# A fused cross-attention and mixture layer: attention probabilities transposed on VectorE in 32x32 blocks instead of on TensorE, with the softmax run one pair of heads ahead

## The chip, the cores and the metric

The kernel runs on one core of one Trainium2 chip. The metric is device time in microseconds (us), the median of three runs. A separate execution of the same program, recorded by the hardware profiler, gives the views quoted below. Engines are named as in the profile: PE is TensorE, PEld its weight loads, DVE is VectorE, ACT is ScalarE, POOL is GpSimd, SP is SyncE, which here only issues DMAs.

## What is computed

```
x: (16, 64, 512)   ctx: (16, 64, 512)   fside: (16, 32, 64, 64)   mask: (16, 64, 64)   all float32 but the mask
n = layernorm(x);  q = n @ Wq;  k = ctx @ Wk;  v = ctx @ Wv          # 32 heads of 128
score = q k^T / sqrt(128) + fside;  masked;  probs = softmax(score)   # 64x64 for each of 16 samples and 32 heads
x = x + (probs @ v) @ Wo
x = x + layernorm(x) @ base_W^T + base_b + routed low-rank term       # 8 experts of rank 16
```

There are 16 samples of 64 tokens, so 1024 rows. The reference works in float32, and the kernel keeps that accuracy with split operands: each operand of a large product is written as hi + lo, and each product is three matmuls (hi*hi, hi*lo, lo*hi).

## The kernel before, in words

**Stages.** Up to about 329 us the kernel makes all keys and values, with a Winograd-like scheme that forms a 2x2 block product from seven sub-products (`winograd`, L207), and stores them in DRAM (`kd`, `vd`). Then comes the attention loop over 16 pairs of heads (NP = 16), from 329 to about 728 us. The last stage is the dense layer with its router.

**The step strings.** In the attention loop the order of TensorE's work is written out by hand, one letter for a step:

- Q is one of the seven sub-products of the queries of the *next* pair (six 512-column matmuls, `Queries.run`, L514 to L538). Sub-products 1, 6, 7 and 4 add up in one PSUM bank, x, and after each of them ScalarE copies the bank out (`u`, L530, or `q`, L533) before the next of them may write it. Sub-product 2 has bank z; 5 and 3 share bank y. VectorE adds the copies to z or y (`q`, L537).
- S is the scores of both heads of a pair (`scores`, L455): 64 recorded matmuls, then for each head on VectorE scale and bias (L465) and the negated maximum (L467), on ScalarE eight exponentials with their sums (L470), and on VectorE the reciprocal and the normalising product (L473 to L475). A pair's two heads are called A and B below.
- T turns one head's probabilities: four TensorE transposes of 128x128 into a bank (L481) and a ScalarE copy into SBUF (`pt`, L484).
- O is one of the eight token blocks of the output projection of the *previous* pair (six 512-column matmuls, `proj_o`, L501), added to the accumulator `acc` by VectorE (L510).

Between the strings stands the product of probabilities and values (`pv_mm`, L487), called PV here: 128 recorded small matmuls for both heads into four banks, each bank then split by ScalarE (`oh`, L70) and VectorE (`ol`, L71). The strings are "QSQQQQQTQT" for the first pair, "QSQQOOQOQOOQOQOTTO" for the middle ones and "SOOOOOOTOT" for the last. A pair's probabilities are thus used in the same turn in which they are made.

**What sets the order.** On each engine instructions run in the order fixed when the program is built; a scheduler places them by priority and dependence, and an instruction that waits holds everything behind it on its engine. SP issues all loads in one such queue: keys (`load_k`, L426), values (`load_v`, L433), Wo (`load_o`, L440), the side bias (`bias_of`, L450), Wq (`load_pair`, L413). GpSimd adds the mask to the bias (L453) and forms sums of Wq blocks (L161). Buffers come from tagged pools whose sizes are in BLOCKS (L40): `sn` (8) holds `u`, `p` and `pt`, `v` (5) the value blocks. There are six large PSUM banks (`psp`) and two small ones (`pss`), which hold the scores and the transposes.

**After the loop** the weights of the dense layer are split into hi and lo (`bh`, `bl`, `lbh`, `lbl`, L70 and L71).

Of the kernel before, what the change touches and what calls it, by code (L numbers as in the profile page):

```python
# [9 lines left out]
F32 = mybir.dt.float32  # L10
# [9 lines left out]
P = 128  # L20
D = 512
# [17 lines left out]
ORDER_1 = (1, 6, 5, 7, 2, 4, 3)  # L39
BLOCKS = dict(raw=10, g=18, sum=4, sn=8, ob=8, v=5, bm=2, o=9)  # L40
BIG = 1.0e30
# [6 lines left out]
def xattn_ffn_kernel(ctx: ExitStack, tc: tile.TileContext, x, ctxT, wq, wk, wv, wo, fside, mask,  # L48
# [20 lines left out]
    def split(hi, lo, src, lo_eng=None):  # L69
        nc.scalar.copy(hi, src)  # L70
        (lo_eng or nc.vector).tensor_tensor(lo, src, hi.bitcast(F32), ALU.subtract)  # L71

# [36 lines left out]
    with ExitStack() as actx:  # L109
# [6 lines left out]
        def small_bank(name):  # L116
            return pss.tile([P, 512], F32, tag="s", name=name)
# [208 lines left out]
        def x_turn(t, xn):  # L326
            ps = small_bank("pst")
            transposed(ps, xn)
            b, g = divmod(t, 4)
            dst = xT.rearrange("p k (g a b s) -> p g b k a s", g=4, a=2, b=2)[:, g, b]  # L330
            nc.scalar.copy(dst, ps.rearrange("p (k a s) -> p k a s", k=KC, a=2))

# [14 lines left out]
        with tc.manual_schedule(engines={nc.tensor.engine}):  # L347
# [75 lines left out]
            def gran_q(rq, order):  # L423
                return Weights(rq[0][:, 0], rq[0][:, 1], rq[1][:, 0], rq[1][:, 1], P, nc.gpsimd).all(order)

            def load_k(h):  # L426
                kT = []
                for j in range(2):
                    kT.append(blk("raw", "kT"))
                    nc.sync.dma_start(out=kT[j], in_=kd[h][:, j * HALF:(j + 1) * HALF])  # L430
                return kT
# [24 lines left out]
            def scores(qT, kT, bm):  # L456
                ps = small_bank("pss").rearrange("p (t s) -> p t s", t=NT)
                for t in range(NT):
                    for a in range(2):
                        n = 4 * (t // 2) + 2 * a + t % 2  # L460
                        c = slice((n % 8) * S, (n % 8 + 1) * S)
                        nc.tensor.matmul(ps[a * S:(a + 1) * S, t, :], lhsT=qT[n // 8][:, c],  # L462
                                         rhs=kT[n // 8][:, c], start=True, stop=True)
                p = blk("sn", "p", F32, (P, NT, S))
                nc.vector.scalar_tensor_tensor(p, ps, scale, bm, ALU.mult, ALU.add)  # L465
                nm = sm.tile([P, NT], F32, tag="nm", name="nm")
                nc.vector.tensor_reduce(nm, p, AX.X, ALU.max, negate=True)  # L467
                sme = sm.tile([P, NT], F32, tag="sme", name="sme")
                for t in range(NT):
                    nc.scalar.activation(p[:, t, :], p[:, t, :], AF.Exp, bias=nm[:, t:t + 1],  # L470
                                         accum_out=sme[:, t:t + 1])
                rc = sm.tile([P, NT], F32, tag="rc", name="rc")
                nc.vector.reciprocal(rc, sme)  # L473
                nc.vector.tensor_tensor(rc, rc, valid, ALU.mult)  # L474
                nc.vector.tensor_tensor(p, p, rc.unsqueeze(2).to_broadcast([P, NT, S]), ALU.mult)  # L475
                return p

            def transpose_p(p):
                ps = small_bank("pst")
                for g in range(4):  # L480
                    nc.tensor.transpose(ps[:, g * P:(g + 1) * P],  # L481
                                        p[:, 2 * g:2 * g + 2, :].rearrange("p t k -> p (t k)"), ident)
                pt = blk("sn", "pt", F32, (P, NT, S))
                nc.scalar.copy(pt, ps.rearrange("p (u q) -> p u q", q=S))  # L484
                return pt

            def pv_mm(i, pt, v, home="o"):  # L487
                ps = [bank() for _ in range(2)]
                for u in range(NT):
                    for b in range(2):  # L490
                        r = slice(b * S, (b + 1) * S)
                        for d in range(0, P, S):
                            c = slice(i * P + d, i * P + d + S)
                            nc.tensor.matmul(ps[b][d:d + S, u * S:(u + 1) * S], lhsT=v[u // 2][r, u % 2, c],  # L494
                                             rhs=pt[r, u, :], start=True, stop=True)
                res = []
                for b in range(2):
                    hl = [blk(home, f"o{c}", F32R) for c in "hl"]
                    split(hl[0], hl[1], ps[b])
                    res.append(hl)  # L500
                return res  # L501

            def proj_o(t, cts, w):
                ps = bank()
                b, g = divmod(t, 4)
                c = slice(g * P, (g + 1) * P)
                for i, ct in enumerate(cts):
                    mm3(ps, [a[:, c] for a in ct[b]], w[i], i == 0, i == 1)
                with tc.high_priority(offset=SOON):
                    nc.vector.tensor_tensor(acc[:, t, :], acc[:, t, :], ps, ALU.add)  # L510

            class Queries:
# [6 lines left out]
                def run(self, g, order):  # L519
                    mm = mm_weights(tx, g)  # L520
                    b, s = {}, {}
                    for i in order:
                        x_ = "x" if i in (1, 6, 7, 4) else "z" if i == 2 else "y"
                        if i in (1, 2, 5):
                            b[x_] = bank()
                        mm(i, 0, b[x_], i in (1, 2, 5))
                        with tc.high_priority(offset=SOON):
                            if i in (1, 6, 7):
                                s[i] = blk("sn", "u")
                                nc.scalar.copy(s[i], b["x"])  # L530
                            if i == 4:
                                self.blocks[1, 0] = blk("ob", "q21")
                                nc.scalar.copy(self.blocks[1, 0], b["x"])  # L533
                            for at, key, u, bk in ((2, (0, 0), 1, "z"), (7, (1, 1), 7, "y"), (3, (0, 1), 6, "y")):
                                if i == at:
                                    self.blocks[key] = blk("ob", "q")
                                    nc.vector.tensor_tensor(self.blocks[key], s[u], b[bk], ALU.add)  # L537
                        yield  # L538
# [22 lines left out]
            NP = H // 2  # L561
            pts = v = w = prev = None
            for p in range(NP):
                last = p + 1 == NP
                if pts is not None:
                    prev = ([pv_mm(i, pts[i], v) for i in range(2)], w)
                v = load_v(p)
                after = None
                steps = "SOOOOOOTOT" if last else "QSQQOOQOQOOQOQOTTO" if p else "QSQQQQQTQT"
                pts, t, n = [], 0, 0  # L570
                for c in steps:
                    if c == "S":
                        ps = [scores(qs.head(i), ks[i], bms[i]) for i in range(2)]
                        if not last:
                            ks = [load_k(2 * p + 2 + i) for i in range(2)]
                            bms = [bias_of(2 * p + 2 + i) for i in range(2)]
                    elif c == "Q":
                        nxt(1)
                        n += 1
                        if n == 3:  # L580
                            w = load_o(p)
                        if n == 7 and p + 2 < NP:
                            after = Queries(load_pair(p + 2), ORDER)
                        if n == 7 and p + 2 == NP:
# [7 lines left out]
                            for kc in range(KC):  # L592
                                nc.sync.dma_start(out=sbw[kc], in_=base_wT[:, kc])
                    elif c == "T":
                        pts.append(transpose_p(ps[len(pts)]))
                    else:
                        proj_o(t, *prev)
                        t += 1
                        if last and t == 2:
                            w = load_o(p)  # L600
                qs, nxt = nxt, after
            now = ([pv_mm(i, pts[i], v, "g") for i in range(2)], w)
            proj_o(t, *prev)
# [10 lines left out]
    bl = fw.tile([P, KC, NF], F32R, name="bl")  # L614
    for i in range(2):
        split(bh[:, 2 * i:2 * i + 2, 0:NB], bl[:, 2 * i:2 * i + 2, 0:NB], sar[i])
    for kc in range(KC):
        split(bh[:, kc, NB:NF], bl[:, kc, NB:NF], sbw[kc])
    lbh = fw.tile([P, NF], F32R, name="lbh")
# [202 lines left out]
```

## Time and profile before

| What | Value |
|---|---|
| Median of three runs | 777.97 us (777.95 to 778.37) |
| The profiled execution's own time | 779.41 us |
| Span of its records | 777.6 us |
| Granted TensorE clock | 0.997 of full |
| One middle pair, from S to the next S | 25.81 us (371.20, 397.01 and 422.82 us in the chain) |
| PE busy | 770.8 us |
| DVE, ACT, POOL busy | 574.3, 413.6, 134.9 us |
| DMA engines' mean share | 46.7% |

The span begins with the first recorded instruction and ends with the last. Busy time is the union of an engine's records, waits left out. Matmuls are pipelined, so a record of 390 ns starts about 227 ns after the one before it; what a matmul costs TensorE is this distance, not its record.

### The profile page before, as it was taken

The numbers are of one execution on the slowest core, as the hardware profiler recorded it, in microseconds if no ns is written. First come the engines' busy times: TensorE is split into PE (matmuls) and PEld (weight loads), VectorE is DVE, ScalarE is ACT, GpSimd is POOL, SyncE is SP. The second block draws the span as 40 slices with busy tenths as digits, with TensorE's granted clock in tenths as the row PEclk, the third lists the DMA queues.
The fourth block names the chain that finished last, engine by engine and source line by source line (L and its number), as shares of the span: only waits on it lengthen the run. The fifth ranks groups of instructions, "written<-read, shape, count | busy, mean of one in ns | idle before, by whom it ended". The sixth has DMA issues, their size and how long they took to land.

```text
span 777.6 us, 16694 instructions
## 1 busy us (share of the span) xinstructions
PE 770.8 (99%) x6314; PEld 642.1 (83%) x6314; DVE 574.3 (74%) x1036; ACT 413.6 (53%) x1165; POOL 134.9 (17%) x143
## 2 busy tenths in 40 slices
PE   8999999999999999999999999999999999999998
PEld 6888887888888888887888888888888888888898
DVE  6986666665665756787877787778777877779875
ACT  5664454545454545575564556455645564556461
POOL 0000000000000522133330332033203320310330
PEclk9999999999999999999999999999999999999999
DMA  6695646464536345474554355435543544352011
GB/s 243 227 294 179 195 161 209 131 208 151 203 120 204 122 140 200 166 243 140 185 164 122 110 178 165 129 104 176 164 138 96 176 164 131 103 176 70 1 53 58
DMA packets 74705, 120.48 MB, mean 155 GB/s; under 512 B 7680, under 2 KB 24832, under 8 KB 74624
## 3 DMA queue, kind: packets, MB, share of 16 engines
q1 hardware_dynamic: 74480, 119.36, 46.7%
q8 instruction: 49, 0.80, 0.4%
q14 instruction: 32, 0.26, 0.1%
q10 hardware_dynamic: 144, 0.06, 0.0%
HBM read 83.74 MB, written 35.65 MB: 154 GB/s over the span
## 4 chain that ended last, share of the span: by engine, by line
PE 95%; DVE 3%; ACT 1%; DMA 1%; issue 0%; POOL 0%; SPq 0%; DVEq 0%; ACTq 0%; POOLq 0%
PE ps L259 74%; PE yz L259 5%; PE ps L668 5%; PE pss L462 4%; PE ps L494 4%; PE pst L481 2%; DVE gl L71 1%; ACT p L470 1%; DMA cT<-in_ctxT 1%; PE pst L104 0%; DVE bs L634 0%; DVE wl L71 0%; PE pt L104 0%; DVE ol L71 0%; DVE acc L510 0%
## 5 line engine op out<-in xcount | busy, mean ns | idle before, releaser
L70 ACT CAST gh<-s 128x512 fp32r<-128x512 f32 (+1 forms) x128 | 65.6, 515 | 121.1 <-PE ps L259 112.3
L470 ACT ACTIVATE p<-p,nm 128x64 f32<-128x64 f32 x256 | 85.5, 336 | 31.3 <-DVE nm L467 31.3
L259 PE MATMUL ps<-wh,oh 128*128 128x512 f32 x256 | 101.3, 396 | 0.0
L510 DVE TENSOR_TENSOR acc<-acc,ps 128x512 f32<-128x512 f32 x128 | 85.9, 681 | 20.2 <-PE ps L259 20.0
L259 PE MATMUL ps<-wh,ol 128*128 128x512 f32 x256 | 99.8, 390 | 0.0
L259 PE MATMUL ps<-wl,oh 128*128 128x512 f32 x256 | 99.8, 390 | 0.0
L71 DVE TENSOR_TENSOR gl<-s,gh 128x512 fp32r<-128x512 f32 (+1 forms) x128 | 71.5, 562 | 32.9 <-ACT gh L70 31.8
L161 POOL TENSOR_TENSOR s<-rq 128x256 f32<-128x256 f32 x32 | 27.6, 863 | 262.8 <-DMA rq<-in_wq 127.9
L71 DVE TENSOR_TENSOR gl<-raw,gh 128x512 fp32r<-128x512 f32 x48 | 34.5, 722 | 36.5 <-ACT gh L70 26.1
L259 PEld LDWEIGHTS ps<-wl,oh 128*128 128x128 f32 x256 | 48.0, 188 | 10.0
L259 PEld LDWEIGHTS ps<-wh,ol 128*128 128x128 f32 x256 | 48.1, 188 | 9.7 <-DVE ol L71 0.4
L259 PEld LDWEIGHTS ps<-wh,oh 128*128 128x128 f32 x256 | 48.1, 188 | 9.5
L70 ACT CAST gh<-raw 128x512 fp32r<-128x512 f32 x48 | 29.7, 622 | 48.3 <-PE yz L259 29.3
L453 POOL TENSOR_TENSOR bm<-bm,maskb 128x512 f32<-128x512 f32 x32 | 48.2, 1526 | 28.9 <-DVE rc L474 21.5
L470 ACT ACTIVATION_READ_ACCUMULATOR p<-p,nm 128x1 f32 x256 | 48.2, 188 | 0.0
L71 DVE TENSOR_TENSOR ol<-ps,oh 128x512 fp32r<-128x512 f32 x64 | 39.9, 682 | 10.3 <-ACT oh L70 10.3
L96 POOL TENSOR_TENSOR rs<-rs,nhalf 128x1 f32<-128x1 f32 x8 | 4.4, 551 | 246.1 <-DVE rs L95 246.1
L537 DVE TENSOR_TENSOR q<-u,ps 128x512 f32<-128x512 f32 x48 | 32.6, 680 | 9.2 <-PE ps L259 8.9
L70 ACT CAST oh<-ps 128x512 fp32r<-128x512 f32 x64 | 33.2, 591 | 11.6 <-PE ps L494 11.6
L71 DVE TENSOR_TENSOR gl<-rq,gh 128x256 fp32r<-128x256 f32 x48 | 26.9, 562 | 15.4 <-ACT gh L70 15.4
L462 PEld LDWEIGHTS pss<-kT,q 128*64 128x64 f32 x1024 | 31.3, 138 | 5.7 <-PE ps L259 5.2
L475 DVE TENSOR_TENSOR p<-p,rc 128x512 f32<-128x512 f32 x32 | 34.9, 1092 | 1.1
(260 smaller groups left out, 2015.8 us busy)
## 6 DMA issues: line engine op xcount, KB each, us to landing
kd<-c SPq DMA_DIRECT2D x64, 256.0 KB, 2.2
vd<-c SPq DMA_DIRECT2D x64, 256.0 KB, 2.6
kT<-kd SPq DMA_DIRECT2D x64, 256.0 KB, 5.0
v<-vd SPq DMA_DIRECT2D x64, 256.0 KB, 4.3
raw<-in_wk SPq DMA_DIRECT2D x32, 256.0 KB, 4.0
raw<-in_wv SPq DMA_DIRECT2D x32, 256.0 KB, 4.1
rq<-in_wq SPq DMA_DIRECT2D x32, 256.0 KB, 4.7
bm<-in_fside SPq DMA_DIRECT2D x32, 256.0 KB, 5.0
```

The lines of the kernel that those rows point to most:

```text
L70: nc.scalar.copy(hi, src)
L71: (lo_eng or nc.vector).tensor_tensor(lo, src, hi.bitcast(F32), ALU.subtract)
L161: self.eng.tensor_tensor(r, a, b, op)
L259: nc.tensor.matmul(o, lhsT=a, rhs=b, start=first and n == 0, stop=last and n == 2, skip_group_check=True)
L453: nc.gpsimd.tensor_tensor(bm, bm, maskb, ALU.add)
L462: nc.tensor.matmul(ps[a * S:(a + 1) * S, t, :], lhsT=qT[n // 8][:, c], rhs=kT[n // 8][:, c], start=True, stop=True)
L470: nc.scalar.activation(p[:, t, :], p[:, t, :], AF.Exp, bias=nm[:, t:t + 1], accum_out=sme[:, t:t + 1])
L475: nc.vector.tensor_tensor(p, p, rc.unsqueeze(2).to_broadcast([P, NT, S]), ALU.mult)
L494: nc.tensor.matmul(ps[b][d:d + S, u * S:(u + 1) * S], lhsT=v[u // 2][r, u % 2, c], rhs=pt[r, u, :], start=True, stop=True)
L510: nc.vector.tensor_tensor(acc[:, t, :], acc[:, t, :], ps, ALU.add)
L537: nc.vector.tensor_tensor(self.blocks[key], s[u], b[bk], ALU.add)
L668: nc.tensor.matmul(o, lhsT=a, rhs=b, start=start, stop=stop, skip_group_check=True)
```

## The change

- **The turn.** TensorE's transposes and the copy out of PSUM are gone. `turned_p` now makes one VectorE transpose per head that turns each 32x32 block in place (`pb`), then one ScalarE copy of the whole of `pb` into `pt`, then four SBUF-to-SBUF DMAs of 32 partitions x 1 KB that put the two off-diagonal blocks of each half where they belong.
- **The tokens.** So that each half of the partitions holds one sample, the order of tokens in `x`, `ctx` and the output is changed on the host side, and the indexing in `x_turn`, `scores` and `pv_mm` follows. The number and size of these instructions stay.
- **The order.** `scores` is cut into `scores`, `exps` and `normed`. In the step strings the scores of a pair now come at the top of a turn, PV (letter P) is inside the string and uses the probabilities made in the turn before, h stands for normalising and turning one head, e for one head's exponentials, and a small o for a projection step of the pair before the previous one. New ordering edges (`issue_after`) put groups of instructions behind others on the same engine: Wo's split behind the split of PV's banks, the second head's exponentials behind the copy of sub-product 7, the dense layer's weight splits behind the turn of pair 14's last head. The splits of PV's banks get high priority.
- **Buffers.** `sn` grows from 8 to 9, `v` shrinks from 5 to 4.

Matmul records fall by 128 and SP's DMA issues rise by 128; VectorE has 32 transposes more, ScalarE has as many instructions as before.

```diff
-BLOCKS = dict(raw=10, g=18, sum=4, sn=8, ob=8, v=5, bm=2, o=9)
+BLOCKS = dict(raw=10, g=18, sum=4, sn=9, ob=8, v=4, bm=2, o=9)
...
-            def transpose_p(p):
-                ps = small_bank("pst")
-                for g in range(4):
-                    nc.tensor.transpose(ps[:, g * P:(g + 1) * P],
-                                        p[:, 2 * g:2 * g + 2, :].rearrange("p t k -> p (t k)"), ident)
-                pt = blk("sn", "pt", F32, (P, NT, S))
-                nc.scalar.copy(pt, ps.rearrange("p (u q) -> p u q", q=S))
+            def turned_p(p):
+                pb = blk("sn", "pb", F32, (P, 2, NT, 32))
+                turned[:] = [nc.vector.transpose(pb, p.rearrange("p t (b k) -> p b t k", b=2))]
+                pt = blk("sn", "pt", F32, (P, 2, NT, 32))
+                turned.append(nc.scalar.copy(pt, pb))
+                with tc.issue_after(loaded[-1].ins):
+                    for r in (0, S):
+                        for a in range(2):
+                            to, at = r + 32 * (1 - a), r + 32 * a
+                            nc.sync.dma_start(out=pt[to:to + 32, a], in_=pb[at:at + 32, 1 - a])
                 return pt
...
-                steps = "SOOOOOOTOT" if last else "QSQQOOQOQOOQOQOTTO" if p else "QSQQQQQTQT"
+                steps = ("QSQQQQQQ" if p == 0 else "SQQQPQQOOQOhOQOOOO" if p + 2 < NP else
+                         "SQQQPQQQQOhSeeOOOOOh" if p + 1 < NP else "PoohOOOOOOO")
...
+                    if c == "P":
+                        old, told = prev, t
+                        prev, t = ([pv_mm(i, pts[i], v, "g" if p + 1 == NP else "o") for i in range(2)], w), 0
+                        del pts[:2]
+                        v = load_v(p)
+                    elif c == "S":
+                        ss += [scores(pairs[ns].head(i), ks[i], bms[i]) for i in range(2)]
+                        ns += 1
...
+                        if p == ns - 1:
+                            exps_of(1 if p else 2)
+                        if p == 0:
+                            soften()
+                            soften()
                     elif c == "Q":
+                        nxt = pairs[p + 1]
                         nxt(1)
                         n += 1
-                        if n == 3:
-                            w = load_o(p)
+                        if n == 5 and ss:
+                            with tc.issue_after(nxt.third):
+                                exps_of(1)
+                                soften(nxt.last)
+                        if n == 5:
+                            with ExitStack() as behind:
+                                for e in [e.ins for e in evicted] or [nxt.first]:
+                                    behind.enter_context(tc.issue_after(e))
+                                w = load_o(p)
...
+                    elif c == "h":
+                        soften(added.ins)
+                    elif c == "e":
+                        behind = list(turned)
+                        with tc.issue_after(turned[1].ins):
+                            exps_of(1)
+                    elif c == "o":
+                        added = proj_o(told, *old)
+                        told += 1
...
+    with tc.issue_after(behind[0].ins), tc.issue_after(behind[1].ins):
+        for i in range(2):
+            split(bh[:, 2 * i:2 * i + 2, 0:NB], bl[:, 2 * i:2 * i + 2, 0:NB], sar[i])
```

`exps_of(n)` runs the exponentials of n heads that wait in `ss`; `soften` runs `normed` and `turned_p` for the next head.

## The prediction

> **What bounds the kernel now.** I read first the busy line and the shares of the chain that ended last.
>
> ```profile
> PE 770.8 (99%) x6314; PEld 642.1 (83%) x6314; DVE 574.3 (74%) x1036; ACT 413.6 (53%) x1165; POOL 134.9 (17%) x143
> ...
> PE 95%; DVE 3%; ACT 1%; DMA 1%; issue 0%; POOL 0%; SPq 0%; DVEq 0%; ACTq 0%; POOLq 0%
> ```
>
> TensorE is busy for all but 7 us, and the chain runs through it. So work taken from TensorE is worth its full time if nothing makes TensorE wait afterwards. Next the chain through one middle pair (start, length, what):
>
> ```profile
> 391.14 0.87 PE pst L481 x8
> 392.02 1.38 PE ps L259 x6
> 393.39 2.02 PE ps L494 x128
> 395.42 1.59 PE ps L259 x6
> 397.01 2.02 PE pss L462 x64
> 399.02 17.93 PE ps L259 x78
> 416.96 0.87 PE pst L481 x8
> ```
>
> The pair takes 25.81 us, with no other engine in the chain. The eight transposes take 0.87 us, a step of six large matmuls 1.36 to 1.38. The engine's waits add one thing, TensorE's only wait in the whole attention loop, at 361.6 us:
>
> ```profile
> PE ps L259 <- DVE q L537: 0.7, 1, 0.7
> ```
>
> Then the busy time by stage, one pair (length, then PE, PEld, DVE, ACT, POOL):
>
> ```profile
> 371.20:397.00 25.80, 25.80 (x292) 21.45 (x293) 20.45 (x36) 14.16 (x52) 6.48 (x6) 1.00 0.43 142
> ```
>
> VectorE has 5.3 us to spare in a pair, ScalarE 11.6. Last, ScalarE's timeline in the first pair, and the rows nearest to the new work:
>
> ```profile
> 331.81 0.35 ACT L470 ACTIVATE p<-p,nm 128x64 f32<-128x64 f32 x1 [1.96 <-DVE nm L467]
> ...
> 332.16 0.33 ACT L470 ACTIVATE p<-p,nm 128x64 f32<-128x64 f32 x1
> ...
> 333.16 0.56 ACT L530 COPY u<-ps 128x512 f32<-128x512 f32 x1
> ```
>
> ```profile
> L475 DVE TENSOR_TENSOR p<-p,rc 128x512 f32<-128x512 f32 x32 | 34.9, 1092 | 1.1
> L467 DVE TENSOR_REDUCE nm<-p 128x8 f32<-128x512 f32 x32 | 22.0, 686 | 1.0
> L484 ACT COPY pt<-pst 128x512 f32<-128x512 f32 x32 | 17.4, 587 | 23.6 <-PE pst L481 23.6
> ```
>
> Exponentials start 0.334 us apart. After four of them the copy of a sub-product (u) gets its turn; that interleaving is what keeps TensorE fed there, and it will matter.
>
> [...] the ordinary one-input row here is 686 ns for 512 elements. No transpose on VectorE is in this trace. [...] the same product p<-p,rc takes 0.68 us at best and 1.81 at worst, while GpSimd works.
>
> **The change, part by part.**
>
> *Transposes off TensorE.* The first and last pair spend 2 x 0.44 us on them, the fourteen others 0.87: 0.88 + 0.88 + 14 x 0.87 = 13.9 us saved, switching included, since these are distances along the chain. PV and S still stand between large matmuls as often as before, so no other switch appears. The wait at 361.6 us should go too, because its cause was the crowded second pair: -0.7.
>
> *VectorE transposes.* 32 x 0.69 = 22 us, 1.4 a pair: 20.45 + 1.4 = 21.8 us in a pair of 24.9. Off the path at that price. [...] I take 0.69. [...]
>
> *ScalarE copy.* 0.59 us for each head as now, from SBUF in place of PSUM: nothing.
>
> *DMAs.* Eight a pair, 32 KB each. SP takes 0.32 to 0.4 us to issue one, and the shortest landing on the page is 2.2 us (kd<-c), so a head is home about 4 us after its copy. In the new order they are issued behind the second half of the next keys and one Wo load; what is queued behind them is the other Wo load, needed some 12 us later, and the next pair's Wq, bias and keys, which cannot go before the next S anyway. The later head is turned near 22 us after S, home near 26, used at 31: 5 us of slack. Nothing. In bytes it is 4 MB on 120.
>
> *The tokens, the value buffers.* The same count of instructions; four value blocks are refilled right behind PV, 23 us before use. Nothing.
>
> *The new order in a middle pair.* Counted from S: Q1 at 2.02, Q2 at 3.5, Q6 at 4.87, PV at 6.3, then Q5, Q7, and the first O at 11.2. Two places are tight. Q6 writes bank x again and must wait for the copy of Q1. In the first pair of the kernel before scores started at 329.10, the copy began at 333.16 and took 0.56: 4.62 after S, 0.2 us early, if VectorE is free at 1.2 us. I walked VectorE's order: it has caught up by the seventh O with about 0.5 us to spare, so yes. The first O needs the split of PV's banks; ScalarE begins 1.1 us after PV's start (now 523.58 against 522.46), so VectorE's first split ends near 8.7: early. I allow 0.05 us a pair: +0.6. The bounds are 0 and about 0.3.
>
> *The filling, a new wait.* In the first turn all sixteen exponentials, both copies to pt, two Wo casts and a Wq cast stand ahead of the copy of Q6 on ScalarE; Q7, two steps later on TensorE, waits for that copy. TensorE: S at 329.10, Q6, Q5, ready for Q7 at 333.97. ScalarE: exponentials from 331.81, 16 x 0.334, to 337.15; copy for A 0.5, casts 0.5 + 0.5 + 0.3, to 339.0. Head B meanwhile: last sum ready 337.3, reciprocal and products to about 338.4, one Wo split to 339.05, transpose to 339.75; copy for B to 340.3, then the copy of Q6 to 340.9. TensorE stands from 333.97 to 340.95: +7.0, bounds 6.3 (no VectorE contention) to 9 (GpSimd's bias addition and a slow transpose). Then S of the second pair follows Q3 directly, and its second quarter needs VectorE's sum of Q3, behind two small splits: +0.9 (0.5 to 1.5). Nothing hides these 7.9 us: on TensorE everything stands behind Q7.
>
> *The draining.* In turn 14 Q4 follows Q7 with no O between, while ScalarE still has four splits and two Wo casts ahead of the copy of Q7: ready at 12.0 against 11.2 us after S, +0.8. In turn 15 VectorE also carries six splits of the dense weights (0.4 to 0.7 us each), so PV's split for the first O comes late, about +0.6; and the last head's transpose near 38 us after S of turn 14, plus copy and DMAs, meets the last PV at 40.3 to 41.3, about +1.0. Sum +2.4, bounds 0.8 to 6. The moved splits leave the window 720 to 740 us, where TensorE hardly waits (0.3 us), so nothing comes back.
>
> *Sum*, on the profiled execution: 779.41 - 13.9 - 0.7 + 0.6 + 7.9 + 2.4 = 775.7 us. The runs' median lies 1.44 below that execution, so 777.97 - 3.7 = **774.3 us**.
>
> **The rivals.**
> - *Clean.* Neither filling nor draining costs anything: 777.97 - 13.9 - 0.7 = 763.4. For it: TensorE waits almost nowhere now, and every order is by hand. Against: ScalarE's order in the first turn is fixed, and 16 x 0.334 us cannot shrink.
> - *Slower: VectorE's transpose at half pace.* Each pair has two; at 1.37 us VectorE carries 1.36 us more. Half a us of slack before the seventh O and 0.2 at Q6 absorb 0.6, the rest, 0.73 us, holds Q6 in each of 13 pairs: 9.5 us. With the 0.6 already allowed taken out: 774.3 - 0.6 + 9.5 = 783.2. It decides from about 1.2 us a transpose, where 13 pairs lose 4 us. For it: VectorE stands at 21.8 of 24.9 us already. [...]
> - *A wash.* One cost alone at its upper bound: filling 10.5 us (776.9), draining 6 us (777.9), or 0.3 us lost at Q6 in each of 13 pairs (777.6).
> - That TensorE does the transposes still is excluded: 128 of its matmuls are gone from the changed program.
>
> **How the numbers follow.** Differences within 0.2% (776.4 to 779.5 us) are about what a measurement of this kernel can tell from no change. The forecast, 770 to 776.4: 0.62. Clean or nearly, below 770: 0.10. Wash: 0.14. Slower, above 779.5: 0.14. So faster 0.72, same 0.14, slower 0.14. The range 766 to 780 leaves out about 0.05 below and 0.12 above; the transpose at 1.37 us lies outside it.
>
> **What would show it.** No pst records from L481, and S to S at 24.9 us in the middle pairs. A gap on TensorE of 7 us near 334, ended by ScalarE's copy u, and VectorE's transpose at 0.69 us. If the middle pairs keep a wait at Q6 or at the first O, the walk of VectorE's order is wrong; if the gap near 334 is absent, my reading of ScalarE's order is. If PV waits for a DMA in the middle pairs, the slack of 5 us was wrong.

## The result and the profile after

| | before | after |
|---|---|---|
| Median | 778.27 us (777.47 to 779.87, 21 runs) | 776.67 us (775.14 to 778.86, 21 runs) |
| Ratio | | 0.998, 95% interval 0.9972 to 0.9987 |
| Span of the profiled execution | 777.6 us | 774.9 us |
| From the first scores to the end | 777.6 - 329.10 = 448.5 us | 774.9 - 327.90 = 447.0 us |

The kernel became 1.6 us faster; 3.7 were forecast. Of the two spans' difference of 2.7 us, 1.2 lie before the first scores, in the keys stage. The change leaves that stage's work as it is, and its end varies between executions anyway (327.42 to 329.38 us over the changed kernel's experiments below). What is left, 1.5 us, is the size of the median's gain, so the account below starts at the first scores. Of the 21 runs after, the eleven with a mean granted clock of 0.996 took 775.14 to 776.67 us, the ten with 0.993 to 0.995 took 776.68 to 778.86.

The busy line and the granted clock of the page after:

```profile
PE 758.6 (98%) x6186; PEld 629.7 (81%) x6186; DVE 556.0 (72%) x1068; ACT 416.4 (54%) x1165; POOL 123.0 (16%) x143
...
PEclk9999999999999999989999999999999999999999
```

TensorE works 12.2 us less, but the span fell by 2.7 us only, so waits took most of it. One slice of the clock row is an 8: the 18th of 40, 329 to 349 us, which is the first turn.

The chain through a middle pair after (start, length, what):

```profile
399.39 2.02 PE pss L464 x64
401.40 4.33 PE ps L259 x18
405.73 2.04 PE ps L511 x128
407.77 16.52 PE ps L259 x72
```

Scores, three sub-products, PV, twelve steps, and the next scores at 424.29: 24.90 us, with no other engine and no transposes. The middle pairs take 24.90 to 24.98 us (one takes 25.85), where 25.81 stood before.

TensorE's waits after (total, times, longest):

```profile
PE ps L259 <- ACT u L548: 7.9, 2, 7.2
...
PE ps L259 <- DVE ol L71: 0.8, 1, 0.8
PE ps L259 <- issue: 0.8, 1, 0.8
...
PE ps L511 <- DMA pt<-pb: 0.5, 1, 0.5
...
PE pss L464 <- DVE q L559: 0.4, 1, 0.4
```

The first line holds the wait of 7.2 us in the first turn and one of 0.7 in turn 14; "issue" is idle time for which the profile shows no cause. ScalarE's timeline there shows what stands ahead of the copy u of sub-product 6 when the sixteenth exponential is through:

```profile
335.92 0.60 ACT L494 COPY pt<-pb 128x512 f32<-128x512 f32 x1
336.43 1.13 ACT L70 CAST wh<-so 128x512 fp32r<-128x512 f32 x2
337.47 0.40 ACT L70 CAST gh<-rq 128x256 fp32r<-128x256 f32 x1
338.98 0.62 ACT L494 COPY pt<-pb 128x512 f32<-128x512 f32 x1 [1.10 <-DVE pb L492]
339.50 0.58 ACT L548 COPY u<-ps 128x512 f32<-128x512 f32 x1
```

This is the queue that the prediction named: sub-product 6 is complete near 331.6 us, but its copy starts at 339.50, behind everything that stands ahead of it on ScalarE. What the prediction didn't name comes next, on TensorE. In its timeline the distance of starts is what counts:

```profile
332.31 0.39 PE L259 MATMUL ps<-t5h,gl 128*128 128x512 f32 x1
332.54 0.39 PE L259 MATMUL ps<-t5l,gh 128*128 128x512 f32 x1
340.13 0.80 PE L259 MATMUL ps<-t7h,gh 128*128 128x512 f32 x1 [7.21 <-ACT u L548]
340.73 0.63 PE L259 MATMUL ps<-t7h,gl 128*128 128x512 f32 x1
341.15 0.63 PE L259 MATMUL ps<-t7l,gh 128*128 128x512 f32 x1
341.58 0.63 PE L259 MATMUL ps<-t7h,gh 128*128 128x512 f32 x1
```

Before the wait a matmul starts 0.23 us after the one before it. After it the first distance is 0.60, the next ones are 0.42 to 0.43 up to 344.56, and one more is 0.40. The four sub-products from the restart to the next scores take 7.89 us (340.13 to 348.02); in experiment 1, at full pace, they take 5.69. So the wait cost its own 7.2 us and 2.2 us more.

The trace shows the granted clock itself. In the next view a line is a stretch of time, with its length and the busy time of PE, PEld, DVE, ACT and POOL; the third figure from the end is the granted TensorE clock:

```profile
334.66:338.08 3.42, 0.00 (x0) 0.00 (x0) 2.58 (x5) 3.21 (x13) 2.38 (x3) 1.00 0.90 314
338.08:341.49 3.41, 1.36 (x3) 1.16 (x4) 1.44 (x3) 1.10 (x2) 3.33 (x4) 0.50 0.40 116
341.49:344.91 3.42, 3.42 (x9) 2.64 (x8) 1.02 (x2) 1.50 (x4) 0.00 (x0) 0.50 0.39 120
344.91:348.32 3.41, 3.41 (x24) 2.56 (x24) 2.32 (x6) 1.56 (x4) 0.00 (x0) 1.00 0.24 61
```

The clock was at half from 338.08 to 344.91 us: behind an idle stretch, and until a stretch full of work was over. Of these 6.8 us TensorE worked the last 4.8, from 340.13 on; they are the slow phase. Experiments 1, 9 and 11 will show that shorter waits can bring it (2.33 us in 1, 1.00 and 0.65 us in 11), and that the length alone doesn't decide (1.8 us in 9 didn't).

The groups of the new turn, and its DMAs (KB each, median us to landing):

```profile
L492 DVE STREAM_TRANSPOSE pb<-p 128x512 f32<-128x512 f32 x32 | 22.6, 705 | 0.1
L483 DVE TENSOR_TENSOR p<-p,rc 128x512 f32<-128x512 f32 x32 | 22.1, 689 | 0.6
L494 ACT COPY pt<-pb 128x512 f32<-128x512 f32 x32 | 19.9, 621 | 25.1 <-DVE pb L492 18.7 <-issue 5.9 <-DMA kT<-kd 0.2
...
pt<-pb SPq DMA_DIRECT2D x128, 32.0 KB, 1.9
```

The transpose takes 0.705 us. The normalising product fell from 1.09 to 0.69 us on average at its new place.

### The profile page after: what moved, and what is told of

Same layout as the page of the kernel before. It is cut to its first block, busy times and chain, and to the rows that moved or that the text cites. A ratio compares the mean times of both kernels' runs of the same rounds, so it can differ in the third digit from the quotient of the medians.

```text
span 774.9 us, 16651 instructions
## 1 busy us (share of the span) xinstructions
PE 758.6 (98%) x6186; PEld 629.7 (81%) x6186; DVE 556.0 (72%) x1068; ACT 416.4 (54%) x1165; POOL 123.0 (16%) x143
## 4 chain that ended last, share of the span: by engine, by line
PE 91%; DVE 3%; issue 2%; ACT 2%; DMA 1%; SPq 1%; POOL 0%; DVEq 0%; ACTq 0%; POOLq 0%
PE ps L259 73%; PE yz L259 5%; PE ps L727 5%; PE pss L464 4%; PE ps L511 4%; DMA cT<-in_ctxT 1%; ACT p L475 1%; PE pst L104 0%; DVE bs L693 0%; DVE bl L71 0%; PE pt L104 0%; ACT wh L70 0%; DVE acc L528 0%; DVE s L161 0%; DVE ol L71 0%
## 5 line engine op out<-in xcount | busy, mean ns | idle before, releaser
L161 POOL TENSOR_TENSOR s<-rq 128x256 f32<-128x256 f32 x32 | 24.6, 768 | 266.6 <-DMA rq<-in_wq 226.9
L455 POOL TENSOR_TENSOR bm<-bm,maskb 128x512 f32<-128x512 f32 x32 | 41.5, 1316 | 28.7 <-DMA bm<-in_fside 28.7
L70 ACT CAST gh<-rq 128x256 fp32r<-128x256 f32 x48 | 19.5, 406 | 37.3 <-PE ps L259 33.4
L548 ACT COPY u<-ps 128x512 f32<-128x512 f32 x48 | 27.9, 580 | 20.7 <-PE ps L259 11.6
L511 PEld LDWEIGHTS ps<-pt,v 64*64 64x64 f32 x2048 | 32.0, 135 | 6.2 <-issue 5.9
```

The source lines that it names most:

```text
L70: first = nc.scalar.copy(hi, src)
L161: self.eng.tensor_tensor(r, a, b, op)
L455: nc.gpsimd.tensor_tensor(bm, bm, maskb, ALU.add)
L511: nc.tensor.matmul(ps[a][d:d + S, t * S:(t + 1) * S], lhsT=v[t // 2][r, t % 2, c], rhs=pt[r, :, t, :], start=True, stop=True)
L548: copy = nc.scalar.copy(s[i], b["x"])
```

## The experiments

Theory (clock): the gain that is missing is mostly in the first turn, the wait and the slow pace after it. Rival (spread): it is many small waits. Each kernel was timed beside the kernel before, whose medians were 778.59 (experiments 1 to 4), 778.12 (5 to 8) and 777.96 us (9 to 12).

**1. TensorE kept busy during the wait.**

```diff
                         nxt(1)
                         n += 1
+                        if p == 0 and n == 3:
+                            d = small_bank("pss")
+                            for _ in range(56):
+                                nc.tensor.matmul(d[:, 0:256], lhsT=zero[:, 0:P], rhs=zero, start=True, stop=True)
```

> The changed kernel with 56 extra matmuls on zeros (bf16, 256 columns, into a bank of scores that nobody reads then) ahead of sub-product 7 in the first turn, so that TensorE works while it waits there. The end of the wait, set by ScalarE's copy u, doesn't move. Theory (clock): the changed kernel lost 2.4 us after the wait, because after 7.2 us of idling twelve large matmuls came 0.43 us apart in place of 0.227. With TensorE kept busy they come 0.227 apart from the first on: -2.4 us against the changed kernel, about 774.2 us, ratio to before 0.995. The extra matmuls, 0.114 us each at full pace, end near 339.2, before the copy does. Rival (spread): the slow matmuls are an effect of traffic or of the operands, and the missing time is the sum of small waits elsewhere: no gain, 776.7 us, ratio 0.998, and the matmuls behind the wait still come 0.43 us apart.

Measured: 776.95 us median (774.02 to 782.75, 22 runs), ratio 0.998 (0.9968 to 0.9992). The pace is as the theory has it. TensorE's timeline:

```profile
337.75 1.25 PE L627 MATMUL pss<-zero 128*128 128x256 bf16 x10
340.18 0.50 PE L259 MATMUL ps<-t7h,gh 128*128 128x512 f32 x1 [1.18 <-ACT u L548]
340.52 0.40 PE L259 MATMUL ps<-t7h,gl 128*128 128x512 f32 x1
340.75 0.40 PE L259 MATMUL ps<-t7l,gh 128*128 128x512 f32 x1
```

The copy comes at the same time, and the matmuls behind it start 0.23 us apart: scores to scores in the first turn fell from 20.12 to 18.02 us. The mean granted clock is 0.997 or more in 19 of these 22 runs, and at most 0.996 in all 21 after, so this isn't one execution's chance. Yet the median didn't move. The profiled execution shows one place where the gain went, the last PV:

```profile
711.21 1.28 PE L511 MATMUL ps<-pt,v 64*64 64x64 f32 x68
714.82 1.97 PE L511 MATMUL ps<-pt,v 64*64 64x64 f32 x60 [2.33 <-DMA pt<-pb]
716.72 0.79 PE L259 MATMUL ps<-wh,oh 128*128 128x512 f32 x1
717.31 0.63 PE L259 MATMUL ps<-wh,ol 128*128 128x512 f32 x1
```

There the last head's DMA landed late, and another slow phase followed (mean granted clock 0.82 from 716 to 722 us): from the last PV to the end 63.2 us, 59.9 after, 59.3 before. This isn't all of it, for the three runs with a mean clock of 1.000 took 774.02 to 777.25 us. The pace was shown, its worth in time not yet.

**2. The first turn in the order of the middle ones.**

```diff
+                        if p == 0:
+                            half = ss.pop(0)
+                            half = (*half, exps(*half, ts=range(4))[1])
-                        if p == ns - 1:
-                            exps_of(1 if p else 2)
-                        if p == 0:
-                            soften()
-                            soften()
+                        elif p == ns - 1:
+                            exps_of(1)
...
+                        if p == 0 and n == 2:
+                            with tc.issue_after(nxt.second):
+                                soft.append(exps(*half, ts=range(4, NT)))
+                        if p == 0 and n == 4:
+                            soften(nxt.third)
```

(`second` is the copy of sub-product 6; Wo's split of this turn goes behind the next pair's Wq.)

> The changed kernel with the first turn ordered as the middle ones: four exponentials of head A, the copy of sub-product 6, the other four, the copy of 7, then head B's exponentials; each head is turned after them, and Wo's split goes to the end of the turn. Theory (clock and order): the wait of 7.2 us goes, and with it the slow restart of 2.4 us and the 0.4 us before the next scores; head B is then turned late, near 341.5, and its DMAs land about 345.5, so the first product of probabilities and values waits 0 to 1.5 us. Gain 8.5 to 10 us against the changed kernel: 767 to 768 us, ratio 0.986. Rival (order alone): the slow restart is no consequence of the wait; gain 7.2 at most, 769.5 us or more. Second rival (the wait moves): what leaves sub-product 7 comes back in front of the first product of probabilities and values; gain under 4 us, over 772.7.

Measured: 768.71 us (767.75 to 769.28), ratio 0.9874 (0.9861 to 0.9887): 8.0 us less than after, a little less than expected. ScalarE now copies u after four exponentials, at 332.19, and the first turn takes 10.43 us from scores to scores; the clock stays at full in the whole loop (0.999 on average over the execution). The second turn grew from 26.37 to 28.07 us: part came back there, in a wait of 0.86 us before a sub-product and two of PV for its DMAs (0.16 and 0.93 us).

**3. VectorE's transpose twice, 4. the small DMAs twice.**

```diff
+                nc.vector.transpose(pb, p.rearrange("p t (b k) -> p b t k", b=2))
                 pt = blk("sn", "pt", F32, (P, 2, NT, 32))
```
```diff
-                            nc.sync.dma_start(out=pt[to:to + 32, a], in_=pb[at:at + 32, 1 - a])
+                            for _ in range(2):
+                                nc.sync.dma_start(out=pt[to:to + 32, a], in_=pb[at:at + 32, 1 - a])
```

> The changed kernel with each VectorE transpose run twice into the same tile, so 1.4 us of VectorE per head in place of 0.7. By the walk in the prediction, which gave VectorE some 0.7 us to spare in a middle pair at its tight places, this holds the sixth sub-product up by 0.73 us in each of 13 pairs: +9.5 us, 786 us. Theory now: in the changed kernel's middle pairs VectorE is busy 18.9 us of 24.94, less than the 21.8 of the prediction, because the normalising product fell from 1.09 to 0.69 us; so the second transpose is covered, and only the first turn pays, 0.7 us for the transposes ahead of the copy u: 777.4 us, within 1 us.

> The changed kernel with each of the eight small DMAs of a pair issued twice. SP takes 0.35 to 0.6 us for each, so a head is home 1.5 to 2.5 us later, and what stands behind in SP's queue goes out 3 to 5 us later in a pair. Prediction and theory now: the slack of 5 us and the queue's idle time cover it in the middle pairs; only the last pair, which waited 0.5 us for its probabilities, waits 2.5 us more: 779 us, S to S still 24.94. Rival: SP's queue is the tight one, loads of keys or Wo come late and the middle pairs grow by 0.3 us or more: over 781 us.

Measured: 781.2 us, ratio 1.0039 (1.0026 to 1.0052), and 785.76 us, ratio 1.0102 (1.0084 to 1.012). Both cost more than the theory said, but mostly not where the rivals said. The chain of a middle pair with two transposes per head:

```profile
400.44 2.02 PE pss L464 x64
402.45 4.32 PE ps L259 x18
406.78 2.04 PE ps L512 x128
408.82 16.56 PE ps L259 x72
```

The next scores stand at 425.38: 24.94 us, as after. With the DMAs doubled ten of the twelve middle pairs take 24.89 to 25.03 us, two 26.1 and 26.5; in the first of these PV waits 0.87 us for a DMA. Most of what the two changes cost is at the ends: with the double transpose the first wait grew to 8.3 us and the way from the last PV to the end by 1.8; with the double DMAs the last two PVs came 18.7 us apart, not 15.0.

**5. The end of the loop, 6. both ends** (the edits of 2 and 5 together). The edit of 5:

```diff
-                                for e in [e.ins for e in evicted] or [nxt.first]:
+                                for e in [e.ins for e in evicted] + [nxt.third] * (p + 2 == NP) or [nxt.first]:
...
-                         "SQQQPQQQQOhSeeOOOOOh" if p + 1 < NP else "PoohOOOOOOO")
+                         "SQQQPQQQQOhSeeOOOOOh" if p + 1 < NP else "PohoOOOOOOO")
...
                         v = load_v(p)
+                        behind = list(evicted)
...
-                        behind = list(turned)
```

> The changed kernel with three edits at the end of the loop and the first turn as it is: in turn 14 Wo's split stands behind the copy of sub-product 7, in the last turn head B is turned one projection step earlier, and the dense layer's weight splits stand behind the split of the second-last probability product, not ahead of it. Theory: of the changed kernel's draining 0.72 us is the copy of 7 behind Wo's casts and 0.49 us the last probabilities' DMA; VectorE no longer has six dense splits (3.5 us) between the last maxima and the last transpose, so the last head is home 2 to 3 us earlier, and its DMA may vary without cost. Gain 1.2 us over the profiled run, more on the median, where other runs of this order waited 2.3 us there: 774.5 to 775.5 us, ratio 0.996. Rival: the splits come back ahead of the dense layer, where VectorE works without a pause from 720 to 728 us: no gain, 776.7.

> Reordered first turn and reordered end of the loop together. Theory: the two are independent, gains add: 768.7 less 1.2 to 2 us, 766.7 to 767.5 us, ratio 0.985; TensorE's waits in the loop then sum to under 3 us. Rival: no further gain, 768.7.

Measured: 775.39 us (774.68 to 775.77), ratio 0.9961 (0.9947 to 0.9975), and 767.37 us, ratio 0.9871 (0.9852 to 0.989), both as expected. The last PV no longer waits for its DMA. The wait of 0.72 us before sub-product 4 stayed, although Wo's casts had gone from ahead of the copy, so their queue wasn't its cause.

**7. The order alone, 10. the same with the transposes later.** TensorE's four transposes per head take the place of the VectorE transpose and the DMAs. They don't bring the blocks into the changed order of tokens, so the output isn't the layer's; the amount of work is that of the kernel before.

```diff
+                for g in range(4):
+                    nc.tensor.transpose(pb[:, g * P:(g + 1) * P],
+                                        p[:, 2 * g:2 * g + 2, :].rearrange("p t k -> p (t k)"), ident)
...
-                    later.append([2 if 0 < p < NP - 2 else 0, normed(*soft.pop(0))])     (7)
+                    later.append([4 if 0 < p < NP - 2 else 0, normed(*soft.pop(0))])     (10)
```

> The new order alone: the changed kernel with the four TensorE transposes per head put back (copied from a small PSUM bank), with no VectorE transpose and no DMAs; in the middle pairs they stand two steps behind the point at which the head is normalised. The probability product reads the turned blocks in the changed token order, so the output isn't the reference's; the amount of work is that of the kernel before. Theory: the transposes are worth 13.9 us and the order costs 12: 788 to 791 us, ratio 1.014, S to S 25.8 in the middle pairs, and a wait of about 6 us with a slow restart in the first turn. Rival: the order costs little and the new turn costs what is missing (contention of its DMAs and VectorE's transposes): 780 to 783 us.

> The order alone once more, with the TensorE transposes four steps behind the point of normalising in the middle pairs, not two (output not the reference's, as before). The earlier try had them wait for VectorE's product, 0.5 to 0.9 us in each pair and up to 2.5 at the ends, which says nothing on the order. Theory: with that wait gone in the middle pairs they take 24.94 + 0.87 = 25.8 us; the ends, unchanged, keep some 10 us of waits and slow restarts: 798 to 803 us. Rival: the order itself has a wait in the middle pairs that only shows with TensorE's transposes: S to S stays at 26.6 and more.

Measured: 811.55 us, ratio 1.043 (1.0413 to 1.0447), then 798.52 us, ratio 1.0264 (1.0247 to 1.0281). The first of them missed its forecast: the place chosen for the transposes made TensorE wait in nearly every pair (21.1 us in 19 waits; S to S 26.6 to 27.0 us, once 30.1). The second has S to S at 25.83 to 25.88 in most middle pairs, 0.9 us above after, which is the chain's transposes (two lines of 0.44). Its ends still hold 13.4 us of waits of the transposes' own, in six waits, so its total doesn't price the order.

**8. The turn alone, in the order of before.** The tokens, too, keep the order of before, so the blocks are paired wrongly and the output isn't the layer's; the work is.

```diff
-                ps = small_bank("pst")
...
+                pb = blk("sn", "pb", F32, (P, 2, NT, 32))
+                nc.vector.transpose(pb, p.rearrange("p t (b k) -> p b t k", b=2))
...
+                        nc.sync.dma_start(out=pt[to:to + 32, a], in_=pb[at:at + 32, 1 - a])
```

> The turn alone: the kernel before, in its own order, with VectorE's transpose, the ScalarE copy and the four DMAs in place of TensorE's transposes (sn 9 and v 4 blocks as after; the tokens keep the order of before, so the blocks are paired wrongly and the output isn't the reference's). Theory: a head's probabilities come home 0.7 + 0.6 + 2.4 + 1.9 = 5.6 us after they are normalised, and TensorE has 2.2 us of other work between the place of the transposes and the product that reads them: it waits 3.4 us or more in each of 16 pairs, 54 us, less 13.9: 818 us or more; where the wait is long enough for a slow restart, 2.4 us more each, up to 856. Rival: other work covers the way, 764 us, and running a pair deeper was not needed.

Measured: 783.94 us (783.56 to 785.78), ratio 1.0077 (1.0062 to 1.0093). The theory failed here by 34 us. TensorE's waits:

```profile
PE ps L496 <- DMA pt<-pb: 11.8, 10, 2.9
PE ps L259 <- DVE ol L71: 1.1, 1, 1.1
```

Ten of the thirteen middle distances between scores lie between 24.88 and 24.98 us, as after: in most middle pairs the head is normalised early enough for the way by DMA to be covered without running a pair deeper. The loss lies at the ends (23.4 us from the first to the second scores, 15.1 before; 64.1 from the last PV to the end, 59.3 before) and in three pairs that wait for a DMA. The deeper order brought about 783.94 - 776.67 = 7.3 us, at these places.

**9. Kept busy, with the end of the loop reordered.** The edits of 1 and 5 together.

> The extra matmuls on zeros of the first experiment, together with the reordered end of the loop, so that the last probabilities' DMA no longer decides. The comparison is with the reordered end alone (775.4 us, first turn S to S 20.4 us, twelve matmuls 0.43 us apart). Theory (clock): nothing but the pace after the wait differs, so 2.1 to 2.4 us less: 773.0 to 773.3 us, ratio 0.9935, S to S 18.0 to 18.3. Rival (spread): the first experiment's shorter first turn was luck or is given back elsewhere: 775.4 us.

Measured: 772.23 us (771.5 to 778.99, 9 runs), ratio 0.9932 (0.9912 to 0.9953), 3.2 us under experiment 5. From the restart to the next scores 5.67 us, in experiment 5 8.13: the pace is worth 2.5 us. The copy came 0.7 us later, so 1.8 of it shows in the first turn. The rest of the 3.2 matches a wait of 0.9 us in the second turn for a bank of PV, which this build doesn't have, and a shorter "issue" gap; that these belong to the pace isn't shown. The clock record of this execution has no half stretch in the loop (mean clock 1.000). Nothing reads what the extra matmuls produce.

**11. A projection step moved between sub-products 7 and 4 in turn 14**, on top of experiment 6:

```diff
-"SQQQPQQQQOhSeeOOOOOh"
+"SQQQPQQOQQhSeeOOOOOh"
```

> Both ends reordered, and in turn 14 one projection step between sub-products 7 and 4. In the two runs with the reordered end the wait of 0.72 us before sub-product 4 stayed, though Wo's casts were no longer ahead of the copy; theory: it is the copy itself (0.3 us after the last matmul of 7, and 0.59 long), for which TensorE needs other work. Then 0.7 us less than with both ends reordered: 766.7 us, ratio 0.985. Rival: the wait only moves to the next scores, whose sum comes late: 767.4.

Measured: 766.68 us (766.01 to 768.18), ratio 0.9856 (0.9843 to 0.9869), the lowest median, as expected, though its interval overlaps that of experiment 6. The trace is clearer: turn 14, from scores to scores, fell from 16.40 us (experiment 6) to 15.38 and the wait before sub-product 4 is gone. That wait was the copy's own length. The profiled execution is the longest of the four (768.18) and shows that short waits can bring the slow pace too:

```profile
345.58 1.16 PE L512 MATMUL ps<-pt,v 64*64 64x64 f32 x64
347.75 0.33 PE L512 MATMUL ps<-pt,v 64*64 64x64 f32 x4 [1.00 <-DMA pt<-pb]
348.73 1.15 PE L512 MATMUL ps<-pt,v 64*64 64x64 f32 x60 [0.65 <-DMA pt<-pb]
349.81 0.50 PE L259 MATMUL ps<-t5h,gh 128*128 128x512 f32 x1
350.14 0.49 PE L259 MATMUL ps<-t5h,gl 128*128 128x512 f32 x1
350.43 0.63 PE L259 MATMUL ps<-t5l,gh 128*128 128x512 f32 x1
350.86 0.63 PE L259 MATMUL ps<-t5h,gh 128*128 128x512 f32 x1
```

**12. A shorter wait in the first turn.** Only head A's exponentials and turn stay ahead of sub-product 7:

```diff
-                            exps_of(1 if p else 2)
-                        if p == 0:
-                            soften()
-                            soften()
+                            exps_of(1)
+                        if p == 0:
+                            soften()
```

> The changed kernel with head B's exponentials and turn moved behind the copy of sub-product 7 in the first turn, while head A's copy pt still stands ahead of the copy of 6: the wait before sub-product 7 shrinks from 7.2 us to about 4. Theory (clock): the wait saves 3.2 us; if 4 us still bring the slow restart, 773.5 us with matmuls 0.43 apart behind it, if not, 771. Rival: the saving comes back in front of the first probability product, as head B is turned later: 776.

Measured: 774.2 us (773.74 to 775.79), ratio 0.9953 (0.9941 to 0.9964). The wait was 5.0 us, not 4, because a Wo cast ahead of the copy waited 1.9 us for its DMA; the slow pace followed in full:

```profile
337.52 0.79 PE L259 MATMUL ps<-t7h,gh 128*128 128x512 f32 x1 [5.00 <-ACT u L548]
338.11 0.63 PE L259 MATMUL ps<-t7h,gl 128*128 128x512 f32 x1
338.54 0.63 PE L259 MATMUL ps<-t7l,gh 128*128 128x512 f32 x1
```

The 2.2 us of wait that went brought 2.5 us, so the price of the slow pace didn't shrink with the wait. It follows how long TensorE works at the half clock: 4.8 us after, 5.3 in experiment 5 and 5.5 here, and the four sub-products behind the wait take 2.2, 2.4 and 2.5 us more than at full pace.

## Why the prediction was wrong, and what in it was right

| Term of the sum | forecast | measured |
|---|---|---|
| Transposes off TensorE, wait at 361.6 | -14.6 | -14.6 (0.87 in each middle pair; the wait is gone) |
| Middle pairs, Q6 | +0.6 | 0 (24.94) |
| Filling: wait before sub-product 7 | +7.0 | +7.2 |
| Filling: pace after it | not in the sum | +2.2 |
| Filling: second scores | +0.9 | +0.4 |
| Second turn, a bank of PV | not in the sum | +0.8 |
| Draining: copy of 7, first O, last PV | +0.8, +0.6, +1.0 | +0.7, 0, +0.5 |
| "issue" gap on TensorE near 584 us | not in the sum | +0.8 |
| Sum | -3.7 | -2.0 (-1.5 by the spans) |

- **The step that failed is the filling**, "Nothing hides these 7.9 us": it priced the wait and put what comes behind it at nothing, as if TensorE went on at full pace. Experiments 1 and 9 show the pace as a cost of its own, 2.2 to 2.5 us, by filling the wait with work. It was the largest term that was missing. With it the forecast would have been 774.3 + 2.2 = 776.5. That this lies next to the measured 776.67 is partly luck: the other misses in the table add up to -0.5 us, and 0.5 us is unassigned. The start of the trace before could have told it: its 18 first matmuls, of 256 columns on zeros, take 3.94 us, 0.22 each, as long as 512 columns take later, and from 8.29 to 11.27 us 512-column matmuls, too, start 0.43 us apart, with the clock recorded at half.
- The mechanism of the wait, its place and its size were right, and so was the saving. Experiment 2 shows that wait and slow pace go together when ScalarE's order is mended.
- **The rival of a slow VectorE** is out: 0.705 us a transpose, where the prediction's 0.69 was the author's estimate from the one-input row nm<-p (686 ns), and even 1.4 us per head leave the middle pairs at 24.94 (experiment 3). The prediction had VectorE fuller than it is: it is busy 19.46 us in a middle pair (374.38 to 399.32), not 21.8. Four operations with both operands in SBUF got faster, by 2.4 us a pair together: the product 0.94, Wo's splits 0.62, Wq's 0.43, the small product rc<-rc,valid 0.39. The traces show it go with GpSimd. In the twelve middle pairs before, 20 of the 24 products overlap a record of GpSimd and take 1.25 us on average, the other four 0.69; after, none overlaps and all take 0.68 to 0.70. What couples the two isn't shown; the prediction carried the old times over to an order in which they no longer meet.
- **The slack of 5 us of the DMAs** held in the middle pairs (doubled, the DMAs held up PV in one of twelve, experiment 4), though SP took 0.58 us to issue one and not 0.32 to 0.4. At the ends there is no such slack.
- **Draining**: the sum was too high by 1.2 us, and its first part had the wrong reason: the copy of 7 wasn't late behind Wo's casts, it just had no other TensorE work beside it (experiments 5 and 11).
- **Left open.** 0.5 us between the table and the spans isn't assigned. The "issue" gap isn't explained: it stands in the same pair after and in experiments 2, 3, 5 and 6, 0.7 to 1.3 us long, is 0.3 us or less in 9 (two pairs earlier), 11 and 12, and absent in 1. What makes the runs of one kernel scatter isn't shown either: experiments 5, 6 and 9 share the reordered end, where the last DMA no longer decides, and spread over 1.1, 3.8 and 7.5 us.

## What to carry to other kernels

Price a stall on TensorE at its length plus the slow phase behind it, here 2.2 to 2.5 us in the first turn, and look for it in the granted clock and in the starts of the matmuls that follow. Several short waits close together count as well (experiment 11): in these traces the half clock went with how full TensorE's stretches of 3.41 us were, and each at full clock that was filled to 0.44 or less was followed by one at half. When work is moved off the bounding engine and run a stage deeper, the middle of the loop pays as counted; walk the first and last turn queue by queue, since there the same helper engine serves two heads at once: here that gave back 13 of 14.6 us, and mending the order at both ends brought 10 of them in.

## What the runs showed of the hardware

- The granted clock is recorded as full or half in all 14 traces, and it changes only on a grid of 3.41 us that is fixed within a trace: it is at half from 338.08 to 344.91 us after, two such stretches, and from 8.18 to 11.59 us before, one. From 15 us on, 20 stretches at full clock had TensorE records on 0.44 of their length or less (0.00 after, from 334.66 us; 0.41 before, from 772.76 us), and each was followed by a half stretch; of those with 0.57 or more, none was. In between both occur: 0.49 (after, from 331.25 us), 0.54 (experiment 9, 338.93) and 0.56 (experiment 3, 718.16) stayed full, 0.52 (experiment 7, 542.80) and 0.56 (experiment 11, 346.88) didn't.
- The clock came back only behind a stretch with records on 0.98 or more (1.00 after, 341.49 to 344.91 us); behind 0.78 it didn't (experiments 7 and 8; in 8 it reads 0.50 from 345 to 350 us, with records on 3.63 of the 5 us). In these traces the filling of the stretch tells more than the length of one wait: 2.3 us (experiment 1, last PV) and 1.0 and 0.65 us inside one PV (experiment 11) were followed by the half clock, 1.8 us in experiment 9 and 1.3 us in experiment 3 weren't.
- The product p<-p,rc, with both operands in SBUF, took 0.69 us without a record of GpSimd beside it and 1.25 us on average with one (middle pairs, before). Operations with one operand in PSUM showed no such difference: acc<-acc,ps took 0.68 us in the middle pairs before, with overlap (24 of 96) and without, and ol<-ps,oh 0.68 us in those after, where 47 of 48 overlap.
- With 56 matmuls on zeros in TensorE's first wait (6.29 us) the clock was at full behind it, 1.00 from 340 to 350 us (experiment 1); without them it was at half up to 344.91 us (after).
- The 128 copies of 32 x 1 KB from SBUF to SBUF took SP 0.58 us each to issue and landed after 1.9 us (medians, after), 4.0 at worst.
